# A transformer block on one core: attention starts after 12 projected tiles instead of 16, 22 weight pieces instead of 6 are quantised beside the attention, and the network runs 5 units behind instead of 2

## The chip, the cores and the metric

The kernel runs on one core of one Trainium2 chip. A core has TensorE (PE, the matrix multiplier), VectorE (DVE), ScalarE (ACT), GpSimd (POOL) and SyncE (SP, which here only issues transfers), and each works through its own list of instructions strictly in order; a list stops where an instruction waits for a semaphore. The metric is the device time of one execution in microseconds (us). Three runs of the kernel before took 4254.81, 4255.48 and 4258.41 us; their median, 4255.48 us, is the number that the change is measured against.

## The reference, cut to what matters

For each of 8 sequences of 1024 tokens with 512 features, the layer norm of x feeds two branches whose results are added to x: causal attention with 16 heads of 32 features, and a gated network whose weights and activations are rounded to a 4-bit grid in blocks of 16.

```python
def fp4_linear(x, w):                      # both sides rounded blockwise
    return jnp.einsum('bsk,nk->bsn', fp4_quant_dequant(x), fp4_quant_dequant(w))

def fp4_quant_dequant(x):                  # blocks of 16 along the last dim
    scale = jnp.maximum(jnp.max(jnp.abs(xb), axis=-1, keepdims=True) / 6.0, 1e-12)
    xn = xb / scale
    return grid[searchsorted(mid, abs(xn))] * sign(xn) * scale

xn = layernorm(x)
q, k, v = split(xn @ W_attn + b_attn)      # 512 -> 3 * 512, 16 heads of 32
att = softmax(where(causal, q @ k.T * 32 ** -0.5, -inf))
a = (att @ v) @ W_proj + b_proj
h = silu(fp4_linear(xn, w_gate)) * fp4_linear(xn, w_up)   # 512 -> 1408
out = x + a + fp4_linear(h, w_down)                       # 1408 -> 512
```

## The kernel before

The 8192 tokens are 64 tiles of 128 tokens, 8 to a sequence. The attention of a sequence is 8 units of two heads, so there are also 64 units. Five kinds of work exist, each a generator of small steps:

- `prepare(n)` and `project` (L412 to L532) take a pair of tiles: four transposes each, q and k in four steps (L466) and v in two (L511). q and k are split by DVE into a high and a low part (L491, L492) and stored to memory.
- `maxima(un)` (L557) computes the scores of a unit (PE L597), their row maxima on DVE (L610 for the masked blocks, L622 for the others) and the row sums of the exponentials on ACT (L568). It ends in one small transpose on PE (L655), of which there is exactly one per unit, and in a round trip through memory (L663, L676) that brings the shifts back for `weigh`.
- `weigh(un)` (L682) computes the scores again transposed, takes their exponential on ACT (L735) and multiplies by v (PE L706). While it runs, `maxima` of the next unit runs beside it.
- `network(tiles)` (L785) takes the quantised tile through the gate and up products (L831), SiLU on ACT (L843), the product and the rounding on DVE (L848 and `Quantised`, L267 to L345), transposes (L351) and the down product (L809).
- `finish(tl)` (L914) applies the output projection (L936) to a tile whose whole sequence is through attention, and stores the result.

The network's weights need the same rounding once, before the first tile of the network. They are cut into `PIECES` = 34 pieces of 128 rows by 512 or 384 columns; `weights_quantised` (L357) loads a piece (L367), rounds it on DVE in ten instructions (L335 to L344), turns it on PE (L351) and copies it on ACT (L352).

No engine order is left to a scheduler: `merge` (L1010) takes steps from several `Stream`s in turn and so writes one fixed order for every engine. Each stream has a position that runs with the work done, in units of attention; `merge` picks among the streams that are less than 0.6 units ahead of the last one, with a small model of the engines' costs, to see which could start now. The start is two such merges: the first eight tiles beside weight pieces, then further tiles beside weight pieces and the maxima of unit 0, in the second merge after the loads of units 0 and 1 (`load_half`, 32 transfers at L540, and `load_values`, L552) have been put on SP's list. The third merge holds everything else: unit n at position n, preparations from position 0 on, the network of tile n at position n + `LAG`, `finish` of tile n at n + `LAST` = n + 10. The weight pieces that are left over stand at positions 0 to `LAG` on the network's own stream, ahead of its first tile.

Three constants set the start: `AHEAD` (L76), the number of tiles projected before the third merge; `LAG` (L77); and `EARLY` (L1052), the number of pieces quantised before the third merge. Tiles below `AHEAD` use weights that stay in the chip for that time (L1069 to L1083); later ones fetch them again through a ring of two buffers (`ring_a`, L243).

Of the kernel before, what the change touches and what calls it, by code (L numbers as in the profile page):

```python
# [27 lines left out]
def kernel(  # L28
# [38 lines left out]
    NT = S // P  # L67
# [5 lines left out]
    assert NU == NT  # L73
    QG = 4
    W = QG * P
    AHEAD = 2 * NT  # L76
    LAG = 2  # L77
    LAST = NT + 2
    SOONER = 0.3
    QUEUE = 2.0  # L80
# [76 lines left out]
    def dve(us, after=0.0):  # L157
        return on("dve", us, after)
# [16 lines left out]
    def passed(us):  # L175
        end = clock[0] + us
        while True:
            due = [e for e in waiting_list if e.due <= end]
            if not due:
                break  # L180
            first = min(due, key=lambda e: e.due)
            waiting_list.remove(first)
            clock[0] = max(clock[0], first.due)
            first.now()
        clock[0] = end
# [56 lines left out]

    ring_a = Ring(p2, "wa", wa_in, (B * NT - AHEAD) // QT * 3 * D // (2 * P))  # L243
    ring_p = Ring(p1, "wp", wp_in)
# [112 lines left out]
    def weights_quantised():  # L357
        pieces = []
        for src, dst in ((w_gate, wgT), (w_up, wuT), (w_down, wdT)):
            rows, cols = src.shape  # L360
            for r in range(0, rows, P):
                for c in range(0, cols, CW):
                    pieces.append((src, dst, r, c, min(CW, cols - c)))

        def load(src, dst, r, c, w):
            raw = p3.tile([P, CW], F32, name="hid")[:, :w]
            nc.sync.dma_start(out=raw, in_=src[r : r + P, c : c + w])  # L367
            return raw

        loaded = [load(*piece) for piece in pieces[:3]]  # L370
        done = []
        yield 0.0, clock[0] + 4.0, 0
        for k, piece in enumerate(pieces):
            raw = loaded.pop(0)
            done.append((piece, Quantised(raw, piece[4], raw)))
            while len(done) > (1 if k + 1 < len(pieces) else 0):
                (_, dst, r, c, w), wq = done.pop(0)
                yield from wq.wait()
                transposed(dst[:, c // P : (c + w) // P, r : r + P], wq.done(), w // P)
                if len(pieces) > k + 2:  # L380
                    loaded.append(load(*pieces[k + 2]))
                yield 0.11 * w / P, 0.0, 0, 0.5
# [5 lines left out]
    def load_tokens(tl):  # L388
        tl.xt = p2.tile([P, D], F32, name="xt")
        nc.sync.dma_start(out=tl.xt, in_=x[tl.b, tl.t * P : (tl.t + 1) * P, :])  # L390

    def normed(tl):

        xt = tl.xt
        stats = p4.tile([P, 6], F32, name="stats")
        mv = p4.tile([P, 2], F32, name="mv")
        rstd = p4.tile([P, 1], F32, name="rstd")
        nc.vector.bn_stats(stats, xt)
        nc.vector.bn_aggr(mv, stats)
        nc.vector.tensor_scalar_add(rstd, mv[:, 1:2], EPS)  # L400
        nc.gpsimd.tensor_tensor(rstd, rstd, power, ALU.pow)
        end = pool(0.6, dve(1.1))

        def apply():
            nc.vector.tensor_scalar(xt, xt, mv[:, 0:1], rstd, ALU.subtract, ALU.mult)
            tl.ready = dve(0.57)
            tl.xn = dram.tile([P, D], F32, name="xn_kept", bufs=AHEAD + LAG + 4)
            tl.kept = Later(tl.ready - clock[0] + 0.5, lambda: nc.sync.dma_start(out=tl.xn, in_=xt))

        tl.applied = Later(end - clock[0] + HOP, apply)  # L410

    def prepare(n):  # L412
# [14 lines left out]
        for i, tl in enumerate(tiles[n + QT : n + 2 * QT]):  # L427
            Later(0.5 + i, lambda tl=tl: load_tokens(tl))
            Later(6.0 + 2 * i, lambda tl=tl: normed(tl))
        yield from project(batch, xnT, pair[0].t // QT, end, n < AHEAD)  # L430

    stored = []

    def settle(entries):
        while entries:
            entries.pop(0).now()
# [595 lines left out]
    def up_to(steps, total, over=[0.0]):  # L1032

        total += over[0]
        spent = 0.0
        if steps in said_last:
            yield (0.0,) + said_last[steps]
        while spent < total:
            said = next(steps, None)
            if said is None:  # L1040
                said_last.pop(steps, None)
                return
            said_last[steps] = said[1:3]
            spent += said[-1] if len(said) > 3 else said[0]
            yield said
        over[0] = total - spent
# [2 lines left out]

    N = B * NT  # L1050
    PIECES = sum((w.shape[0] // P) * -(-w.shape[1] // CW) for w in (w_gate, w_up, w_down))
    EARLY = PIECES - 6  # L1052
    tiles = [Tile(n) for n in range(N)]
    units = [Unit(n) for n in range(N)]
    batches = []
# [2 lines left out]
    with tc.manual_schedule(  # L1058
        engines={
            mybir.EngineType.PE,  # L1060
            mybir.EngineType.Activation,
            mybir.EngineType.DVE,
            mybir.EngineType.Pool,
            mybir.EngineType.SP,
        }
    ):
        for tl in tiles[:QT]:
            load_tokens(tl)
        for k in range(2 * NC):  # L1069
            w = p8.tile([P, NC, P], F32, name="pr")  # L1070
            nc.sync.dma_start(out=w, in_=wa_in[:, :, k * P : (k + 1) * P])
            resident_a.append(w)
        nc.sync.dma_start(out=bqk, in_=b_attn[0 : 2 * D].rearrange("(s c p) -> p s c", p=P, c=NC))
        nc.vector.tensor_scalar_mul(bqk[:, 0, :], bqk[:, 0, :], SCALE)
        passed(3.0)
        for tl in tiles[:QT]:
            normed(tl)

        weights_steps = weights_quantised()
        for col in range(2 * D, 3 * D, 2 * P):  # L1080
            w = p2.tile([P, NC, 2 * P], F32, name="wa")
            nc.sync.dma_start(out=w, in_=wa_in[:, :, col : col + 2 * P])
            resident_a.append(w)  # L1083
        part, late = EARLY * 0.25, [0.0]

        def prepared(first, last):
            return itertools.chain(*(prepare(n) for n in range(first, last, QT)))

        merge(
            [  # L1090
                Stream([(prepared(0, NT), 10.8 * NT, 0.0, 1.0)]),
                Stream([(up_to(weights_steps, part, late), part, 0.0, 1.0)]),
            ]
        )
        settle(stored)
        ring_p.load()
        for n, h in ((0, 0), (0, 1), (1, 0), (1, 1)):
            load_half(units[n], h)
        load_values(units[0])
        net = network(tiles)  # L1100
        TILE = sum(4 * 1.72 * w / CW + w / P * 0.97 for _, w in chunks)

        def first_maxima():
            yield 0.0, clock[0] + 6.0, 1
            yield from maxima(units[0])

        merge(
            [
                Stream([(prepared(NT, AHEAD), 10.8 * NT, 0.0, 1.0)]),
                Stream([(up_to(weights_steps, part, late), part, 0.0, 1.0)]),  # L1110
                Stream([(first_maxima(), 6.0, 0.3, 0.7)]),
            ]
        )
        ring_a.load()
        ring_a.load()
        load_biases()

        def last_weights():
            for half in range(2):
                wp = p2.tile([P, NC, 2 * P], F32, name="wa")  # L1120
                nc.sync.dma_start(out=wp, in_=wp_in[:, :, half * 2 * P : (half + 1) * 2 * P])
                resident.append(wp)
            yield 0.0, 0.0, 0

        def networks():
            yield weights_steps, (PIECES - EARLY) * 0.5, 0.0, LAG
            for n in range(N):
                yield up_to(net, TILE), TILE, n + LAG, 1.0

        def preparations():  # L1130
            for n in range(AHEAD, N, QT):
                yield prepared(n, n + QT), 10.8 * QT, n - AHEAD, QT
            yield last_weights(), 1.0, N - AHEAD + 1, 0.0

        merge(
            [
                Stream((weigh(un), 17.5, un.n, 1.0) for un in units),
                Stream((maxima(un), 6.0, un.n - 1 - SOONER, 1.0) for un in units[1:]),
                Stream(networks()),
                Stream((quantised(tl), 0.45, tl.n + LAG - 1, 0.5) for tl in tiles),  # L1140
                Stream(preparations()),
                Stream((finish(tl), 4.5, tl.n + LAST, 1.0) for tl in tiles),
            ]
        )
        passed(100.0)
# [37 lines left out]
```

## Time and profile before

One execution was taken by the profiler. It is not one of the three timed runs.

| what | value |
|---|---|
| median of 3 runs | 4255.48 us |
| the profiled execution, its own time | 4251.42 us |
| its span, first to last instruction | 4249.7 us |
| PE busy | 4131.2 us, 97% |
| DVE busy | 2763.2 us, 65% |
| ACT busy | 2321.8 us, 55% |
| mean granted TensorE clock | 0.991 |
| first statistics transpose (L655) starts | 272.7 us |
| first `weigh` of unit 0 (L724) starts | 290.8 us |
| last weighted product (L706) ends | 4127.2 us |

How to read it: the busy time of an engine is the time in which it has an instruction under way; ends of matmuls are modelled, so a busy PE is not PE at its best rate. The 40 slices of the page are 106 us each. The windows view gives, for a stretch of time, the busy time of each engine with the number of its instructions, the granted TensorE clock and the share of the transfer engines' time. The timeline merges equal instructions that follow each other; a bracket holds the engine's idle time before them and what ended it. The 64 statistics transposes (L655) cut the span into 65 stages, numbered 0 to 64 below: stage 0 is everything up to the first one, stage 64 everything after the last.

### The profile page before, as it was taken

To read this page: it belongs to the slowest core of one execution; us is meant where nothing else is said; L and a number is where in the kernel's file an instruction comes from. 1 tells how busy PE (TensorE), PEld (TensorE's weight loads), DVE (VectorE), ACT (ScalarE), POOL (GpSimd) and SP (SyncE) were. 2 spreads that over 40 slices of the span, in tenths; PEclk is the share of its full clock that TensorE was granted. 3 is DMA by queue.
4 is the path that set the end of the run, shared out by engine and by line. 5 is a ranking of instruction groups with operands and counts; after the bars stand their busy time and mean duration, and the time that the engine had idled before them with its cause. 6 is when DMAs were issued, how large, how long until landed. Compare 5 with 4: busy or idle time off the path is not lost.

```text
span 4249.7 us, 58555 instructions
## 1 busy us (share of the span) xinstructions
PE 4131.2 (97%) x17684; PEld 2619.1 (62%) x17684; DVE 2763.2 (65%) x7323; ACT 2321.8 (55%) x5918; POOL 546.5 (13%) x1296
## 2 busy tenths in 40 slices
PE   7789999999999999999999999999999999999998
PEld 6666666666666666666666666666666555555555
DVE  6786765666575666575666575666565666667755
ACT  2246556565555565555565555565555666666640
POOL 0001111111111111111111111111111111111110
PEclk9889999999999999999999999999999999999999
DMA  5654434455455455455455455455454433333314
GB/s 183 177 173 129 124 103 120 118 157 157 132 155 150 140 164 153 132 156 151 140 160 155 134 154 149 141 162 153 138 149 131 117 92 94 95 92 93 93 56 126
DMA packets 564187, 573.84 MB, mean 135 GB/s; under 512 B 114976, under 2 KB 420128, under 8 KB 563872
## 3 DMA queue, kind: packets, MB, share of 16 engines
q1 hardware_dynamic: 563872, 570.10, 48.3%
q8 instruction: 142, 2.33, 0.2%
q14 instruction: 173, 1.42, 0.1%
HBM read 400.56 MB, written 169.35 MB: 134 GB/s over the span
## 4 chain that ended last, share of the span: by engine, by line
PE 82%; ACT 7%; DVE 4%; DMA 1%; issue 1%; SPq 0%; ACTq 0%; POOL 0%; DVEq 0%
PE bank L831 26%; PE acc L809 12%; PE bank L466 8%; PE y L706 7%; PE bank L724 6%; PE bank L727 6%; PE bank L597 5%; PE bank L936 5%; PE bank L511 4%; ACT bank L568 3%; PE bank L351 2%; ACT L568 1%; ACT L843 1%; ACT pr L735 1%; DMA ks<-y_kept 1%
## 5 line engine op out<-in xcount | busy, mean ns | idle before, releaser
L568 ACT ACTIVATE bank<-bank,neg 128x512 f32<-128x512 f32 (+3 forms) x1536 | 856.7, 559 | 163.7 <-DVE neg L610 119.8
L735 ACT ACTIVATE pr<-bank 128x512 f32<-128x512 f32 (+3 forms) x1536 | 662.7, 494 | 482.6 <-PE bank L727 478.2
L741 POOL TENSOR_SCALAR_AFFINE_SELECT pr<-pr 128x128 f32<-128x128 f32 x1024 | 393.2, 397 | 3238.3 <-ACT pr L735 3228.9
L610 DVE CUSTOM_DVE_ANT_0 bank<-bank,mask 128x128 f32<-128x128 f32 (+3 forms) x1024 | 501.2, 500 | 469.5 <-PE bank L597 455.7
L724 PE MATMUL bank<-shT,pick 128*128 128x512 f32 (+3 forms) x1536 | 683.8, 453 | 2.7 <-DVE hid L848 1.5
L831 PE MATMUL bank<-wuT,xqT 128*128 128x512 f32 (+1 forms) x1536 | 676.1, 565 | 3.9 <-ACT bank L568 1.0
L809 PE MATMUL acc<-wdT,hqT 128*128 128x512 f32 x1408 | 665.4, 596 | 1.3 <-ACT hqT L352 1.3
L831 PE MATMUL bank<-wgT,xqT 128*128 128x512 f32 (+1 forms) x1536 | 662.9, 561 | 0.0
L597 PE MATMUL bank<-ks,qs 128*128 128x512 f32 (+3 forms) x1536 | 636.2, 475 | 24.7 <-ACT bank L568 21.7
L727 PE MATMUL bank<-qs,ks 128*128 128x512 f32 (+3 forms) x1536 | 516.9, 346 | 0.0
L622 DVE TENSOR_REDUCE neg<-bank 128x1 f32<-128x512 f32 x512 | 345.7, 685 | 186.8 <-PE bank L597 185.6
L597 PEld LDWEIGHTS bank<-ks,qs 128*128 128x128 f32 x1536 | 277.5, 191 | 234.1 <-issue 111.3
L831 PEld LDWEIGHTS bank<-wuT,xqT 128*128 128x128 f32 x1536 | 277.0, 190 | 228.8 <-issue 158.9
L831 PEld LDWEIGHTS bank<-wgT,xqT 128*128 128x128 f32 x1536 | 280.0, 190 | 219.3 <-issue 151.9
L724 PEld LDWEIGHTS bank<-shT,pick 128*128 128x128 f32 x1536 | 290.4, 189 | 155.7 <-issue 78.9
L809 PEld LDWEIGHTS acc<-wdT,hqT 128*128 128x128 f32 x1408 | 255.3, 190 | 197.0 <-issue 183.6
L478 ACT ACTIVATE full<-bank,bqk 128x256 f32<-128x256 f32 x256 | 107.4, 470 | 491.1 <-PE bank L466 409.3
L727 PEld LDWEIGHTS bank<-qs,ks 128*128 128x128 f32 x1536 | 290.6, 189 | 110.6 <-issue 77.1
L466 PE MATMUL bank<-xnT,wa 128*128 128x256 f32 x1536 | 349.8, 381 | 0.9 <-ACT xnT L352 0.6
L466 PEld LDWEIGHTS bank<-xnT,wa 128*128 128x128 f32 x1536 | 288.4, 190 | 55.6 <-issue 18.9
L706 PE MATMUL y<-pr,vs 128*32 128x512 f32 (+3 forms) x3072 | 316.5, 501 | 0.8 <-POOL pr L741 0.8
L568 ACT ACTIVATION_READ_ACCUMULATOR bank<-bank,neg 128x1 f32 x1536 | 315.4, 205 | 0.0
(99 smaller groups left out, 4674.7 us busy)
## 6 DMA issues: line engine op xcount, KB each, us to landing
wa<-in_L_attn_W_attn_dram SPq DMA_DIRECT2D x146, 512.0 KB
qs<-qk_kept SPq DMA_DIRECT2D x512, 128.0 KB
ks<-qk_kept SPq DMA_DIRECT2D x512, 128.0 KB
wp<-in_L_attn_W_proj_dram SPq DMA_DIRECT2D x81, 512.0 KB
qk_kept<-high SPq DMA_DIRECT2D x128, 256.0 KB
qk_kept<-full SPq DMA_DIRECT2D x128, 256.0 KB
y_kept<-yu SPq DMA_DIRECT2D x256, 128.0 KB
yT<-y_kept SPq DMA_DIRECT2D x112, 256.0 KB
```

Of the source, the lines that this page charges most:

```text
L466: nc.tensor.matmul(pq[:, j, :], lhsT=halves[j][:, c, :], rhs=xnT[:, c, :], start=(c == 0), stop=(c == NC - 1),)
L568: nc.scalar.activation(part, part, AF.Exp, bias=neg[:, kind, k + j : k + j + 1], scale=1.0 if kind == 1 else -1.0, accum_out=sums[:, kind, ...
L597: nc.tensor.matmul(sc[:, j * n : (j + 1) * n], lhsT=un.qs[Q][:, r, i * P : (i + 1) * P], rhs=un.ks[h][:, r, :n], start=True, stop=True,)
L610: nc.vector.tensor_tensor_reduce(part, part, mask[:, W - n :], scale=-1.0, scalar=3e38, op0=ALU.add, op1=ALU.min, accum_out=neg[:, kind, k ...
L622: nc.vector.tensor_reduce(neg[:, kind, k : k + 1], sc[:, :n], AX.X, ALU.max, negate=True)
L706: nc.tensor.matmul(y[row : row + HD, q0:], lhsT=un.vs[h][:, jj, r * HD : (r + 1) * HD], rhs=pr[:, q0:], start=(j < 2), stop=(j >= last - 1 ...
L724: nc.tensor.matmul(w[:, q0:], lhsT=pick[:, Q * HU + r, :], rhs=un.shT[:, q0:], start=True, stop=False)
L727: nc.tensor.matmul(w[:, q0:], lhsT=un.ks[h][:, r, jj * P : (jj + 1) * P], rhs=un.qs[Q][:, r, q0:], start=False, stop=True,)
L735: nc.scalar.activation(pr[:, q0:], w[:, q0:], AF.Exp)
L741: nc.gpsimd.affine_select(out=pr[:, q0 : q0 + P], in_=pr[:, q0 : q0 + P], compare_op=ALU.is_ge, fill=0.0, base=0, pattern=[[1, P]], channe ...
L809: nc.tensor.matmul(tl.acc, lhsT=job.hqT[:, j, :], rhs=wdT[:, i, :], start=(i == 0), stop=(i == NI - 1))
L831: nc.tensor.matmul(job.g, lhsT=job.tl.xqT[:, c, :], rhs=wT[:, c, job.i0 : job.i0 + job.w], start=(c == 0), stop=(c == NC - 1),)
```

## The change

`AHEAD` goes from 16 to 12, `LAG` from 2 to 5 and `EARLY` from 28 to 12. The two merges of the start take their share of the early pieces by tiles instead of half each, so 8 of the 12 pieces stand beside the first eight tiles and 4 beside the next four. The ring of projection weights, whose count depends on `AHEAD`, then serves two more pairs of tiles, and the memory buffers of normalised tiles (`AHEAD + LAG + 4`) go from 22 to 21. Nothing else is changed.

```diff
-    AHEAD = 2 * NT
-    LAG = 2
+    AHEAD = 12
+    LAG = 5
...
-    EARLY = PIECES - 6
+    EARLY = PIECES - 22
...
-        part, late = EARLY * 0.25, [0.0]
+        part, late = EARLY * 0.5 / AHEAD, [0.0]
...
                 Stream([(prepared(0, NT), 10.8 * NT, 0.0, 1.0)]),
-                Stream([(up_to(weights_steps, part, late), part, 0.0, 1.0)]),
+                Stream([(up_to(weights_steps, part * NT, late), part * NT, 0.0, 1.0)]),
...
-                Stream([(prepared(NT, AHEAD), 10.8 * NT, 0.0, 1.0)]),
-                Stream([(up_to(weights_steps, part, late), part, 0.0, 1.0)]),
+                Stream([(prepared(NT, AHEAD), 10.8 * (AHEAD - NT), 0.0, 1.0)]),
+                Stream([(up_to(weights_steps, part * (AHEAD - NT), late), part * (AHEAD - NT), 0.0, 1.0)]),
                 Stream([(first_maxima(), 6.0, 0.3, 0.7)]),
```

## The prediction

> **What bounds the kernel now.** I read the page first, then the busy time by stages, then the timelines of the engines at the two ends of the span. The page:
>
> ```profile
> PE 4131.2 (97%) x17684; PEld 2619.1 (62%) x17684; DVE 2763.2 (65%) x7323; ACT 2321.8 (55%) x5918; POOL 546.5 (13%) x1296
> ...
> PE   7789999999999999999999999999999999999998
> ...
> DVE  6786765666575666575666575666565666667755
> ...
> PEclk9889999999999999999999999999999999999999
> ```
>
> PE is the bound over the whole, but not in the first three slices, where it is busy for seven or eight tenths and its clock is below full. Only those slices, and the last, leave something to win. The stages, cut where the statistics transposes (L655) start:
>
> ```profile
> core 0: us, PE busy (x) PEld busy (x) DVE busy (x) ACT busy (x) POOL busy (x), PEclk, DMA share, GB/s
> 0.00:272.70 272.70, 205.65 (x967) 177.31 (x967) 206.58 (x484) 73.76 (x174) 14.72 (x34) 0.91 0.58 176
> 272.70:322.60 49.90, 44.20 (x193) 30.43 (x193) 37.83 (x110) 29.13 (x85) 5.50 (x16) 0.88 0.62 179
> 322.60:358.80 36.20, 33.15 (x150) 22.54 (x150) 24.68 (x76) 25.08 (x78) 4.13 (x15) 0.91 0.53 140
> 358.80:419.80 61.00, 59.41 (x272) 36.87 (x270) 35.05 (x97) 40.15 (x103) 10.70 (x29) 0.97 0.41 117
> 921.60:1049.40 127.80, 127.31 (x550) 80.73 (x549) 81.14 (x219) 72.07 (x184) 17.11 (x40) 1.00 0.54 149
> 4127.20:4208.60 81.40, 74.57 (x219) 38.35 (x220) 43.95 (x91) 9.99 (x17) 2.53 (x2) 1.00 0.26 79
> 4208.60:4249.70 41.10, 31.11 (x129) 24.85 (x127) 16.17 (x31) 0.00 (x0) 0.00 (x0) 0.96 0.76 215
> 290.80:332.70 41.90, 40.06 (x200) 27.05 (x199) 40.32 (x110) 28.86 (x84) 7.04 (x20) 1.00 0.70 201
> ```
>
> Stage 0 (first row) is DVE's: 206.6 us busy against some 189 us of matmuls, if these are counted at the spacing of their starts at full clock (a 128x512 one 0.43 us, a 128x256 one 0.215 us, as in the timeline). Stages 1 and 2, attention without the network, fill no engine on PE's side. Two units with everything in them take 127.8 us (fifth row), of which PE is busy 127.3. From stage 3 on each us of PE work is a us of time. The last row of the fence is the stretch in which DVE is densest, 40.3 of 41.9 us.
>
> One stall in stage 0 decides what follows. VectorE's and SyncE's timelines:
>
> ```profile
> 162.21 0.69 DVE L398 BATCH_NORM_STATS2 stats<-xt 128x6 f32<-128x512 f32 x1 [14.06 <-DMA xt<-in_L_attn_x_dram]
> ```
>
> ```profile
> 138.21 1.90 SPq L540 DMA_DIRECT2D qs<-qk_kept  x4
> ...
> 156.36 0.93 SPq L552 DMA_DIRECT2D vs<-v_kept  x2
> 157.54 0.95 SPq L390 DMA_DIRECT2D xt<-in_L_attn_x_dram  x2
> ```
>
> Between the two merges SP issues 32 loads of units 0 and 1 one after the other (18.2 us), and the next tiles' x queues behind them; DVE, in order, waits 14 us for it. From the first L540 to the arrival it is 24.0 us.
>
> **The change, part by part.** The changed program has the same matmuls and DVE instructions in another order; 20 more loads of 512 KB (12 for the four tiles now projected through the ring, 8 of the output weights), and eight loads fewer of activation tables. I count its instructions by stage and price DVE's at their mean by form: a 512-wide piece is ten instructions, 0.679 + 0.178 + 0.353 + 0.181 + 0.683 + 0.430 + 0.432 + 0.687 + 0.701 + 0.686 = 5.0 us; the maxima of a unit 4 x (0.297 + 0.433 + 0.570 + 0.701) + 16 x 0.141 + 8 x 0.685 = 15.7; its statistics 2.2; a split of q or k 1.13; the norm of a tile 1.56. Neighbours overlap a little: stage 1 sums to 44.3 and was busy 37.8, stage 2 to 29.1 and 24.7, so true need is 0.85 of these sums.
>
> *Stage 0.* Before: 29 pieces, 18 norms, 32 splits, one unit's maxima: 227.8 by means, 272.7 us long. After: 13 pieces (65), 14 norms (22), 24 splits (27), maxima and the rest (20): 134; PE's work falls from 189 to 139, so the two are level. Eight tiles were through PE at 120.4 before; with about five transposed pieces fewer (0.44 us each) I take 118. SP's list no longer has two piece loads waiting for DVE there (before, L540 began 14.7 us after the last store of v), so the 32 loads start at 119.8, and x lands 24.0 us later, at 143.8. Behind that point DVE has 42 us left by means, and before, 111 us by means behind the same point took 110: 186. Bounds: 180 (DVE at its 0.85) and 200 (PE late by the 11.7 us it lost at this place before). **186, a gain of 87.**
>
> *Stages 1 to 6*, in place of 321.5 us, are the units without network. After, DVE has 50.8, 39.2, 48.8, 39.7, 41.7 and 33.4 by means (5, 4, 5, 4, 3 pieces in the first five), PE only 33, 29, 30, 29, 30 and 40 of work, ACT 37 to 39 by means, of which 0.78 was busy in stages 1 and 2. So DVE leads, and pieces that stood beside projections now stand beside maxima. Stage 1: 50.8 x 0.85 = 43.4, and the 12.1 us that DVE was idle in this stage before (10.8 of it for the bias product, L257, which keeps its place): 55.5. Stages 2 to 5: 169.4 x 0.85 = 144.8 busy. Bounds: 0.96 dense, as in the last row of the fence, 150.8; or 11.5 us idle in each, as in stage 2 before (36.2 - 24.7), 190.9. The dense row is the nearest, as it holds four pieces in one unit; but in two of the four stages the list has nothing between L637 and L641, where DVE waited 6.0 us for ACT in stage 2. 150.8 + 12 and a little: 165. Stage 6 is PE's, 39.6 of work and 4 over it: 43.5. **Together 264, 57 less than before, with 84 us less of PE work done.**
>
> *Stages 7 to 63* are bound by PE. They gain two pairs of projections (41.3 us and their transposes) and lose 7.3 of network: 34.1 of work. The pattern by which units alternate changes, 58.2 and 63.5 us of PE work per stage instead of 66.8 and 55.0; the sum of a pair is the same, and the excess of time over work (3.0 per stage) came with blocks of score products, of which there are as many. Bounds +-8 us. **3485.5 + 34.1 = 3519.6.** The added loads lie under PE, where the transfer engines were half busy (0.54); POOL, which masks and adds the bias, was busy 17 of 127.8 us and follows its units.
>
> *Stage 64*, after the last statistics, takes over 99.8 us of PE work, 93 of it network: three more tiles have no attention beside them. In 4127.2 to 4208.6 the network alone lost 8 us of 81 (6.8 of it idle), waiting for rounded activations:
>
> ```profile
> 4175.39 0.55 PE L351 MATMUL bank<-ident,hid 128*128 128x128 f32 x3 [0.93 <-DVE hid L344]
> ...
> 4199.92 0.66 PE L351 MATMUL bank<-ident,hid 128*128 128x128 f32 x4 [2.06 <-DVE hid L344]
> ```
>
> 3.4 us of that are the drain at the end, once in either case; 4.8 on 70 makes 7 us for the 100 added. Against it, eight `finish` at the end, 4.8 us apart for 3.45 of PE work, become four and a half: 4 us back. **170.0 + 99.8 + 3 = 273** (bounds 266 and 285).
>
> **Sum.** 186 + 264 + 3520 + 273 = 4243 for the span, 6.5 under 4249.7. The profiled execution's own time is 1.7 over its span and 4.1 under the median; the same shift gives 4249 us, 0.15% less than 4255.48. About 0.2%, 8.5 us, is what a measurement of this kernel can tell from no change, so this is a forecast of no difference: 87 and 57 won, 34 and 103 given back.
>
> *A rule against the change.* In 336 to 350 us the clock was 0.76 of full, though PE's longest listed wait there was 0.3 us; units without network run at 0.90. The Trainium skill ("TensorE: Matmul & The Clock Gate", Part 1) has the clock halved after an idle window of about 3.4 us. By the rule alone the five units, whose PE waits are short, would keep the full clock; by the row their 30 us of PE work become 33. Both stay under DVE's need, so the sum is the same by either.
>
> **The rivals.**
>
> *Slower: DVE idles in the units without network as it did in stage 2.* For it: maxima pass PE, DVE and ACT in turn, DVE is in order, and ACT has two rows of exponentials to do. Against it: the dense row, and a list in which pieces stand between the maxima. Four stages at 48 instead of 41 are +26: span 4269, time 4275. It turns slower than measurable once DVE idles more than 8.8 us per unit ((165 + 15 - 144.8) / 4).
>
> *Faster: these units run dense to the end.* Stages 2 to 5 at 150.8 and stage 1 with 2 less, stage 0 at DVE's lower bound: -22, time 4227. For it, 40.3 busy of 41.9; against it, the 6.0 us wait at L641 and every stage with a different mix.
>
> *The start shortens less.* The 32 loads keep their place between the merges and the lists now put the first score products among the projections of tiles 8 and 9; PE too, in order, could stop there. 200 for stage 0: time 4263, 0.2% slower.
>
> *The tail is worse than before's.* If each of the eight chunk pairs without attention waits 3 us more, as the worst one did (2.06): +20, time 4269.
>
> **How the numbers follow.** No measurable change 0.33, the dense case 0.35 (with all between), DVE idling 0.20, the start 0.06, the tail 0.06. The last three are the slower side, 0.32. The range goes from just under the dense case, 4224, to past the slower ones, 4284; the likeliest case's own is 4247 to 4264.
>
> **What would show it.** The first L655 near 186 us and x of tile 10 arriving near 144, with a DVE wait of some 15 us before it; six stages of about 55, 38, 46, 39, 41 and 44, DVE over nine tenths busy in 2 to 5; pairs of stages of 127.8 us later on; the last statistics near 3970, 273 from the end, with under 5 `finish` after the last down product. The forecast is wrong if DVE in stages 2 to 5 shows idle times over 9 us each (slower) or under 2 (faster), or if the later pairs differ from 127.8 by more than 0.3 us.

## The result and the profile after

The changed kernel takes 4295.92 us (median; 4292.55 to 4299.85) against 4255.45 us of the kernel before, a ratio of 1.0094 with a 95% interval of 1.0077 to 1.0112. It is 0.94% slower; the forecast was 4249 us, no measurable difference, and its range ended at 4284. The profiled execution has a span of 4296.8 us, 47.1 more than the one of before; by the medians the change costs 40.5, because before's profiled execution was 4.1 us under its median and the one of after (4298.54 us) 2.6 over its own. The accounts by stages below go by the spans.

The page of the kernel after, the same lines as were shown of before:

```profile
PE 4185.4 (97%) x17684; PEld 2626.3 (61%) x17684; DVE 2793.2 (65%) x7323; ACT 2312.0 (54%) x5910; POOL 538.9 (13%) x1296
...
PE   8789999999999999999999999999999999999999
...
DVE  6588666566666575666575666675666576666565
...
PEclk9899999999999999999999999999999999999999
```

On this page nothing looks wrong: the first slice is fuller than before, the last one too, and PE is busy 97% as before. PE is busy 54 us longer for the same 17684 matmuls, and that is the only sign. The view by stages says where. It is the windows view of the kernel after, cut at the starts of the statistics transposes (columns: stretch, length, busy time of PE, of weight loads, DVE, ACT and POOL with the number of instructions, granted clock, transfer share, GB/s):

```profile
0.00:188.20 188.20, 148.58 (x697) 127.17 (x697) 119.44 (x291) 54.33 (x134) 13.38 (x30) 0.95 0.64 193
188.20:246.40 58.20, 47.89 (x214) 32.14 (x214) 44.04 (x120) 31.43 (x89) 7.75 (x20) 0.88 0.59 164
246.40:289.20 42.80, 39.60 (x189) 26.09 (x189) 33.94 (x95) 29.13 (x85) 6.43 (x18) 0.96 0.58 155
289.20:334.20 45.00, 41.18 (x192) 26.51 (x192) 42.17 (x117) 30.68 (x89) 8.23 (x20) 0.96 0.68 185
...
374.10:416.90 42.80, 38.20 (x176) 26.15 (x176) 35.84 (x103) 28.50 (x84) 4.80 (x14) 0.92 0.66 178
416.90:467.90 51.00, 48.50 (x195) 27.94 (x193) 31.61 (x86) 31.23 (x85) 7.13 (x19) 0.90 0.37 94
1120.50:1249.60 129.10, 128.16 (x549) 80.71 (x548) 82.87 (x218) 72.13 (x184) 16.76 (x40) 1.00 0.53 148
1249.60:1380.50 130.90, 129.96 (x550) 81.94 (x550) 82.87 (x219) 72.13 (x184) 16.76 (x40) 0.99 0.54 146
4027.90:4296.80 268.90, 255.53 (x849) 140.72 (x847) 147.79 (x314) 44.87 (x84) 17.49 (x33) 0.98 0.26 77
```

Against the prediction's four stretches:

| stretch | before, us | predicted | after | missed by |
|---|---|---|---|---|
| stage 0 | 272.7 | 186 | 188.2 | +2.2 |
| stages 1 to 6 | 321.5 | 264 | 279.8 | +15.8 |
| stages 7 to 63 | 3485.5 | 3519.6 | 3559.9 | +40.3 |
| stage 64 | 170.0 | 273 | 268.9 | -4.1 |

The two ends came as forecast. Three quarters of the miss lies in the long middle, for which the prediction named no rival. Two full units take 129.1 us there (the row from 1120.50), and every third pair 130.8 (the row from 1249.60, to the nearest tenth), where before had 127.8 each time. PE is busy 128.16 of 129.10 us in them: the loss shows as busy time, not as idle time.

PE's matmuls are the same before and after, so the time can be split into PE's work and the rest. Work counts each matmul at the spacing of starts at full clock, as in the prediction (a pair of score products of 512 columns 0.23 us each). The rest, called loss below, is idle time, half clock and waits that show as busy (the trace can list a matmul as under way while it waits):

| loss, us | before | after | change |
|---|---|---|---|
| stage 0 | 84.1 | 49.4 | -34.7 |
| stages 1 to 6 | 46.8 | 89.2 | +42.4 |
| stages 7 to 63 | 179.7 | 220.0 | +40.3 |
| stage 64 | 24.4 | 23.5 | -0.9 |
| all | 335.0 | 382.1 | +47.1 |

The 34.7 us saved in the start are lost again, and more, in the units without network; the middle loses another 40.3 for a reason of its own.

### The profile page after: what moved, and what is told of

Same layout as the page of the kernel before. It is cut to its first block, busy times and chain, and to the rows that moved or that the text cites. A ratio compares the mean times of both kernels' runs of the same rounds, so it can differ in the third digit from the quotient of the medians.

```text
span 4296.8 us, 58607 instructions
## 1 busy us (share of the span) xinstructions
PE 4185.4 (97%) x17684; PEld 2626.3 (61%) x17684; DVE 2793.2 (65%) x7323; ACT 2312.0 (54%) x5910; POOL 538.9 (13%) x1296
## 5 line engine op out<-in xcount | busy, mean ns | idle before, releaser
L568 ACT ACTIVATE bank<-bank,neg 128x512 f32<-128x512 f32 (+3 forms) x1536 | 859.9, 562 | 149.8 <-DVE neg L610 125.8
L610 DVE CUSTOM_DVE_ANT_0 bank<-bank,mask 128x128 f32<-128x128 f32 (+3 forms) x1024 | 502.4, 499 | 535.7 <-PE bank L597 315.2
L741 POOL TENSOR_SCALAR_AFFINE_SELECT pr<-pr 128x128 f32<-128x128 f32 x1024 | 381.7, 387 | 3203.8 <-ACT pr L735 3194.4
L724 PE MATMUL bank<-shT,pick 128*128 128x512 f32 (+3 forms) x1536 | 655.0, 435 | 3.1 <-ACT bank L568 1.8
L831 PE MATMUL bank<-wgT,xqT 128*128 128x512 f32 (+1 forms) x1536 | 653.3, 560 | 2.9 <-DVE res L941 0.2
L622 DVE TENSOR_REDUCE neg<-bank 128x1 f32<-128x512 f32 x512 | 345.7, 685 | 191.6 <-PE bank L597 190.9
L466 PE MATMUL bank<-xnT,wa 128*128 128x256 f32 x1664 | 389.7, 388 | 3.5 <-ACT bank L568 1.4
L466 PEld LDWEIGHTS bank<-xnT,wa 128*128 128x128 f32 x1664 | 318.6, 194 | 70.2 <-ACT bank L568 15.9
L568 ACT ACTIVATION_READ_ACCUMULATOR bank<-bank,neg 128x1 f32 x1536 | 318.7, 208 | 0.0
## 6 DMA issues: line engine op xcount, KB each, us to landing
qs<-qk_kept SPq DMA_DIRECT2D x512, 128.0 KB
ks<-qk_kept SPq DMA_DIRECT2D x512, 128.0 KB
y_kept<-yu SPq DMA_DIRECT2D x256, 128.0 KB
```

Source lines behind the costliest of these rows:

```text
L466: nc.tensor.matmul(pq[:, j, :], lhsT=halves[j][:, c, :], rhs=xnT[:, c, :], start=(c == 0), stop=(c == NC - 1),)
L568: nc.scalar.activation(part, part, AF.Exp, bias=neg[:, kind, k + j : k + j + 1], scale=1.0 if kind == 1 else -1.0, accum_out=sums[:, kind, ...
L610: nc.vector.tensor_tensor_reduce(part, part, mask[:, W - n :], scale=-1.0, scalar=3e38, op0=ALU.add, op1=ALU.min, accum_out=neg[:, kind, k ...
L622: nc.vector.tensor_reduce(neg[:, kind, k : k + 1], sc[:, :n], AX.X, ALU.max, negate=True)
L724: nc.tensor.matmul(w[:, q0:], lhsT=pick[:, Q * HU + r, :], rhs=un.shT[:, q0:], start=True, stop=False)
L741: nc.gpsimd.affine_select(out=pr[:, q0 : q0 + P], in_=pr[:, q0 : q0 + P], compare_op=ALU.is_ge, fill=0.0, base=0, pattern=[[1, P]], channe ...
```

## The experiments

**First theory: the middle depends on whether `LAG` is even.** Preparations come in pairs of tiles and so repeat every two units. The network of tile n stands at n + `LAG`; with an odd `LAG` the even tile's network meets the other half of a preparation. The rival was that fewer tiles ahead (another phase of the projections and their loads) made the pairs longer.

*lag4*: the kernel after with

```diff
-    LAG = 5
+    LAG = 4
```

> The changed kernel with the network four units behind instead of five; 12 tiles and 22 pieces stay. Theory (the parity of the lag sets the order of the full units: with an even lag a pair of units is written in the same order as before the change): two full units take 127.8 us again instead of 129.1 to 130.9, the clock has no half-rate window in them, and the time is 4250 to 4265 us. Rival (the shorter lead of 12 tiles makes the full units slower, whatever the lag): 129 to 131 us for two units, time 4285 to 4300.

Measured: 4262.9 us, ratio to before 1.0020 (1.0010 to 1.0029), as the theory had it. The pairs take 127.8 us, loss in stages 7 to 63 is 178.8.

*prep_shift*: the kernel after, `LAG` 5, with the preparations one unit later

```diff
-                yield prepared(n, n + QT), 10.8 * QT, n - AHEAD, QT
+                yield prepared(n, n + QT), 10.8 * QT, n - AHEAD + 1, QT
```

> The changed kernel with lag 5, but each pair of tiles from the 13th on prepared one unit later. Theory (what counts is the place of the network relative to the preparation, two units being one period of both): the order of the full units is that of before, 127.8 us for two, time 4250 to 4265. Rival (the odd lag is bad against the units themselves, or the 12 tiles are): 129 to 131 us, time 4285 to 4300.

Measured: 4265.5 us, 1.0024 (1.0014 to 1.0034), half a us over the theory's range and far from the rival's. Pairs of 127.8 (two of 128.0 and 128.1), loss in stages 7 to 63 182.5. So it isn't the number 5, nor the distance of the network: it is how network and preparations stand to each other.

*lag3_only*: the kernel before with

```diff
-    LAG = 2
+    LAG = 3
```

> The kernel before with the network three units behind instead of two and nothing else: 16 tiles ahead, 6 pieces beside the attention. Theory (parity): two full units take 129.1 to 130.9 us, some 18 pairs at 2 us more, so time 4285 to 4300, slower by 0.7 to 1%. Rival (the 12 tiles or the late pieces make the full units slower): 127.8 us for two, time 4250 to 4265.

Measured: 4290.9 us, 1.0087 (1.0072 to 1.0102). Pairs of 129.1 (one of 130.8), loss in stages 7 to 63 212.5, with the 16 tiles and 28 pieces of before in the start. So the smaller number of tiles ahead isn't needed for it. By these three it is shown that parity is worth 33 to 41 us in the middle: 220.0 against 178.8 and 182.5 with the start of after, 212.5 against 179.7 with that of before. The miss there was 40.3.

**Second question: what does PE wait for in the odd order?** The timeline of PE in the kernel after, in the pair at 1120 (first line) and in the next, one of those of 130.8 us:

```profile
1148.00 3.72 PE L466 MATMUL bank<-xnT,wa 128*128 128x256 f32 x16
...
1272.68 1.02 PE L809 MATMUL acc<-wdT,hqT 128*128 128x512 f32 x2
1273.54 0.60 PE L351 MATMUL bank<-ident,xs 128*128 128x128 f32 x4
1274.43 1.95 PE L597 MATMUL bank<-ks,qs 128*128 128x384 f32 x4 [0.29 <-ACT bank L568]
1276.56 0.49 PE L597 MATMUL bank<-ks,qs 128*128 128x512 f32 x1 [0.17 <-DMA xn_kept<-xt]
1277.12 5.41 PE L466 MATMUL bank<-xnT,wa 128*128 128x256 f32 x16
```

Five score products in a row; from the transposes at 1273.54 to the projection at 1277.12 there are 3.58 us, where the matmuls need some 1.5. The listed idle times are 0.29 and 0.17 us only. A bank is one of the buffers into which PE writes its results; in this kernel a matmul takes it again only when the engine that reads it is through. ScalarE's timeline of the same place has the reason for the wait for L568:

```profile
1271.70 0.59 ACT L769 COPY yu<-y 128x512 f32<-128x512 f32 x1 [2.99 <-PE y L706]
1272.31 1.28 ACT L568 ACT_TABLE_LOAD   x1
1273.60 0.66 ACT L568 ACTIVATE bank<-bank,neg 128x512 f32<-128x512 f32 x1
```

ACT stands 2.99 us idle at L769, a copy of the weighted sums that PE has yet to finish; behind it, in order, come a table load and then the exponentials that set score banks free. Summed over every run of score products in stages 18 to 29 (excess over their work, per pair), this one run loses 2.04 us after; the costliest of before (four products, behind two table loads and two SiLU) 1.05, and no other run more than 0.4 in either.

*no_table* and *no_table_before*: is it the table load? Both leave SiLU out.

```diff
-            nc.scalar.activation(job.hid, job.g, AF.Silu)
+            nc.scalar.activation(job.hid, job.g, AF.Identity)
```

> The kernel after, same order, with the identity in place of SiLU at L843, so that ScalarE need not load another table between the network and the exponentials; this leaves out SiLU. Theory that the 1.28 us table load makes the bunched score products of the odd order wait: pairs of two full units fall from 129.1 (130.8 every third) to within 0.5 us of what no_table_before shows. Rival, that the order of PE's work itself costs it (bunched products waiting for VectorE and ScalarE and the clock): the pairs stay 1 us or more above those of no_table_before.

> The kernel before with the identity in place of SiLU at L843, as the counterpart of no_table; this leaves out SiLU. If the table loads cost anything in the even order, its pairs fall under 127.8 us; by both theories they fall by under 0.5, since PE is busy 127.3 of 127.8 there.

Measured, one execution each: 4249.16 us and 4218.09. Pairs 128.1 in the odd order, 126.6 in the even one: a gap of 1.5, so the rival's side by the number. The load is worth the same in both, 1.0 us of a pair of 129.1 and 1.2 of one of 127.8, and both theories missed the second: they had it under 0.5, since PE is busy 127.3 of 127.8 us there. What went altogether in the odd order is the pair of 130.8: no half-rate stretch is left in stages 7 to 63.

*yu_dve* and *yu_dve_before*: take L769 off ScalarE, in the odd order and in the even one.

```diff
-            nc.scalar.copy(yu, y)
+            nc.vector.tensor_copy(yu, y)
```

> The kernel after, same order, with the copy of the weighted sums (L769) on VectorE instead of ScalarE. In its later pairs one run of five score products (L597, behind the transposes of xs) costs 2.0 us more than its matmuls: it waits for banks from L568, and ScalarE stands there in order at L769, idle for 2.99 us, with the table load of L568 behind it. Theory (this wait is what the odd order loses): ScalarE loads the table in that idle time, the pairs fall from 129.1 and 130.8 to 127.9 to 128.3, the half-rate windows go, stages 13 to 48 take 2296 to 2310 us instead of 2332.9, and the time is 4258 to 4275. Rival (another wait comes last there, VectorE's or PE's own): the pairs stay over 128.8 and the time at 4288 or more.

> The same edit in the kernel before. Its costly run of score products (1.05 us a pair) waits behind two table loads and two SiLU, with no L769 among them. Theory: pairs stay at 127.8 within 0.2 and the time at 4245 to 4260. Rival, that L769 on ScalarE costs PE time anywhere: pairs fall by about 1 here too and the time is under 4235.

Measured: yu_dve 4265.8 us, 1.0026 (1.0017 to 1.0035) of before, 30 us under the kernel after. Every pair takes 128.1, stages 13 to 48 take 2305.0 us, no half-rate stretch between 447 and 3662 us. yu_dve_before 4257.0, 1.0003 (0.9993 to 1.0012), pairs of 127.7 and 127.8. All as the theory had it. PE's timeline of yu_dve at the same place:

```profile
1271.82 0.60 PE L351 MATMUL bank<-ident,xs 128*128 128x128 f32 x4
1272.18 1.42 PE L597 MATMUL bank<-ks,qs 128*128 128x384 f32 x4
1273.78 0.50 PE L597 MATMUL bank<-ks,qs 128*128 128x512 f32 x1 [0.18 <-ACT bank L568]
1274.34 1.99 PE L466 MATMUL bank<-xnT,wa 128*128 128x256 f32 x8
```

and ScalarE's:

```profile
1267.01 1.28 ACT L568 ACT_TABLE_LOAD   x1
1268.30 0.66 ACT L568 ACTIVATE bank<-bank,neg 128x512 f32<-128x512 f32 x1
```

The table load now falls into the time in which ScalarE was idle. The first exponential after it begins 3.5 us before the transposes (1268.30 and 1271.82), not 0.06 after them (1273.60 and 1273.54), and from the transposes to the projection it is 2.52 us instead of 3.58: 1.06 less a pair, and with it the half clock is gone. The run now loses 0.98 beyond its work, as much as the costliest run of before. Loss in stages 7 to 63 is 185.7 instead of 220.0.

no_table says what part the load has in it. There ScalarE stands at L769 as long as in the kernel after, but no load follows; its line, and PE's two:

```profile
1261.10 0.59 ACT L769 COPY yu<-y 128x512 f32<-128x512 f32 x1 [2.99 <-PE y L706]
```

```profile
1262.95 0.60 PE L351 MATMUL bank<-ident,xs 128*128 128x128 f32 x4
...
1265.46 0.70 PE L466 MATMUL bank<-xnT,wa 128*128 128x256 f32 x2
```

From the transposes to the projection it is 2.51 us here, and the pairs take 128.1 as in yu_dve. So what delays the run is the wait and the load behind it together; either can be taken away. The gap to no_table_before stays because the costliest run of before stands behind table loads too and goes with them: no run there loses more than 0.4. In all, 34 of the 40.3 us went with L769's move off ScalarE, some 8.5 of them as half clock (five pairs that were 1.7 longer). The 0.3 us by which a pair is still longer than in the even order were not taken apart.

**Third question: why do stages 1 to 6 lose 42 us, and what is a move of pieces or tiles worth alone?**

*ahead12_only*: the kernel after with `LAG` and `EARLY` of before, so that only the four tiles move, and with them the shares of the pieces: some 19 of the 28 stand beside the first eight tiles, 14 before.

```diff
-    LAG = 5
+    LAG = 2
...
-    EARLY = PIECES - 22
+    EARLY = PIECES - 6
```

> Attention begins after 12 tiles; the lag of 2 and the 6 late pieces are those of before. Theory (parity): full units at 127.8 us for two; the start is bound by VectorE with 28 pieces beside 12 tiles and gains little, time 4245 to 4265. Rival (the shorter lead costs in the full units): 129 us or more, time 4280 to 4300.

Measured: 4284.4 us, 1.0070 (1.0055 to 1.0085); pairs 127.8, as the theory had it, but the time is 19 us over its range. It lies in the rival's range, whose reason the pairs rule out. The windows view of its start:

```profile
0.00:265.80 265.80, 170.31 (x763) 144.06 (x763) 194.39 (x462) 64.00 (x151) 12.68 (x30) 0.82 0.51 154
```

42.6 us of PE work less, and the start is only 6.9 us shorter (272.7 before): DVE has its 28 pieces all the same, and the clock falls to 0.82. DVE isn't busy throughout either (194.39 us): it waits 25.8 us for pieces to be loaded, 14.5 in the start of before.

*early22_only*: the kernel before with the pieces alone moved, into two units as `LAG` stays 2.

```diff
-    EARLY = PIECES - 6
+    EARLY = PIECES - 22
```

> The kernel before with one part of the change alone: 12 early pieces instead of 28, so that 22 stand in stages 1 and 2 (VectorE 82.0 and 76.3 us by means there); 16 tiles ahead, LAG 2. Start: PE's 178 us and some 50 over it, 230 instead of 272.7. If the two units are bound by VectorE's work they take about 82 and 70, and stages 0 to 4 together 489 instead of 472: time 4268 to 4278 us. If a piece costs as little here as in the start: 4258 or less. If the chain through ScalarE adds 10 us or more per unit: 4288 or more.

Measured: 4297.2 us, 1.0095 (1.0080 to 1.0110). The start is 49.4 us shorter (223.3), stages 1 and 2 are 91.7 longer (96.3 and 81.5 instead of 49.9 and 36.2). The first of them:

```profile
223.30:319.50 96.20, 58.09 (x258) 40.49 (x256) 70.64 (x181) 35.96 (x97) 9.82 (x20) 0.78 0.47 134
```

DVE is busy 70.64 of 96.2, and the 0.85 of its means, on which both the prediction and the expectation rested (82.0 x 0.85 = 69.7), is right as busy time. But 25 us of the stage are none of it. The third branch of the expectation holds by its time and not by its reason: none of DVE's listed waits in this stage is for ScalarE. They are 10.3 us for the bias product (10.8 in the same stage of before), 4.1 for pieces to be loaded, and one that the stage of before doesn't have, for the load of the bias:

```profile
DVE inv_y L251 <- DMA bv<-in_L_attn_b_attn_dram: 9.9, 1, 9.9
```

In stage 2 DVE is busy 65.35 of 81.5 us and waits 7.4 for score products and 4.8 for pieces.

*light_pieces*: the kernel after, same order, without four of the ten DVE instructions of a piece (L325, L328, L342, L343), those that round the weights.

```diff
-            return [
+            return self.kept([
...
+        def kept(self, steps):
+            n = len(steps) if not self.light else 3
+            return steps[:n] + [(*each[:3], lambda: None) for each in steps[n:6]] + steps[max(n, 6):]
...
-            done.append((piece, Quantised(raw, piece[4], raw)))
+            done.append((piece, Quantised(raw, piece[4], raw, light=True)))
```

> The kernel after, in the same order of instructions on every engine, with the four instructions of each weight piece that form the step of the grid and round to it taken away from VectorE (six of ten are left); this leaves out the rounding of the network's weights. By means VectorE has 39.5, 30.1, 37.9, 31.5 and 35.3 us in stages 1 to 5 in place of 50.8, 39.2, 48.8, 39.7 and 41.7. Theory that VectorE's work sets these stages: stages 2 to 5 (170.6 us in the kernel after) fall by 25 to 30, to 141 to 146, and stage 0 falls too. Rival, that the chain from PE through VectorE and ScalarE and back sets them, with the clock: they fall by under 10 us, to 161 or more.

Measured, one execution: 4281.5 us, 14 under the kernel after. Stages 2 to 5 take 158.2 instead of 170.5, 12.3 less; neither branch, but nearer the rival's 161 than the 146 of the theory. Two of the four rows:

```profile
284.60:324.50 39.90, 37.07 (x192) 25.70 (x192) 32.80 (x97) 30.75 (x89) 6.67 (x20) 1.00 0.77 209
324.50:363.80 39.30, 36.61 (x189) 24.53 (x189) 26.93 (x85) 29.00 (x85) 4.63 (x18) 1.00 0.66 174
```

Of 30.9 us less of DVE busy time (146.4 to 115.6) four tenths came back. All four units now take 38.8 to 40.2 us, however much of that DVE is busy (26 to 33), so it isn't DVE's work that sets them any more. DVE's listed waits in them are 23.0 us for PE's score products (L610, L622) and 13.1 for ACT at L641; in the kernel after they are 9.9 and 7.8. What sets the units, presumably the way of a unit's scores through PE, DVE and ACT and back, was not found out. Some of the 12.3 can be the clock: it is 1.00 in all four stages here, and 0.96, 0.96, 1.00 and 0.92 after, which is at most 6.9 us (0.04 x 42.8 + 0.04 x 45.0 + 0.08 x 42.8, if PE was on the path all that time).

**Last: the change turned round.** If tiles beside DVE's pieces are cheap, more of them belong in the start, with `LAG` even.

*ahead20*: `AHEAD` 20, the rest as before (its fractions of pieces taken by tiles as after).

```diff
-    AHEAD = 12
-    LAG = 5
+    AHEAD = 20
+    LAG = 2
...
-    EARLY = PIECES - 22
+    EARLY = PIECES - 6
```

> The kernel after with LAG 2, 28 early pieces and 20 tiles projected ahead: against the kernel before, only AHEAD goes up by four where the change took it down by four. ahead12_only moved 42.6 us of PE work out of the start and shortened it by only 7 us, because VectorE kept its pieces. Theory (the start is VectorE's, and each tile projected beside it brings some 10.8 us of PE work for little of VectorE's): the start has 231 us of PE work and 243 us of VectorE work by means, so it grows from 272.7 to about 282, and 43 us leave the later stages: 4222 to 4230 us, pairs of later stages at 127.8 as LAG is even. Rival (the start is bound by the chain from loads through PE to VectorE and back, each tile costs its PE time): the start grows by 35 to 43 us, to 310 or so, and the time stays at 4250 to 4260.

Measured: 4231.9 us, 0.9949 (0.9932 to 0.9966) of before, 2 us over the expected range. Its start:

```profile
0.00:285.80 285.80, 242.85 (x1175) 211.69 (x1175) 224.65 (x515) 84.27 (x198) 17.98 (x38) 0.96 0.63 192
```

13.1 us longer than before's for 43 us more of PE work, with the clock at 0.96 instead of 0.91; the loss in stage 0 falls from 84.1 to 54.2. The shares of the pieces moved too (some 11 beside the first eight tiles instead of 14), and DVE's 14.5 us of waiting for pieces to be loaded are gone; what each of these is worth was not taken apart.

*ahead24* (`AHEAD` 24, otherwise as ahead20):

> As ahead20, with 24 tiles projected ahead. VectorE's work in the start stays (241 us by means), PE's grows from 231.6 to 253.7, and stage 1 takes 21 us more of PE work and 17 more of VectorE's; 43 us leave the later stages. If PE's work beside VectorE's goes on being nearly free (ahead20: 43 us of it lengthened the start by 13), the start stays under 295 and the time is 4210 to 4220. If the start has become PE's by now, it grows by 22, stage 1 by 21, and the time stays at 4228 to 4236.

Measured: 4231.9 us, 0.9938 (0.9922 to 0.9955). The start is 12.1 longer again, but stage 1 takes 79.2 instead of 52.1: the branch without further gain holds, though it is stage 1 and not the start that gives back the most.

*ahead20_e3* (ahead20 with `EARLY = PIECES - 3`):

> As ahead20, with 31 pieces in the start instead of 28: three pieces, 14 us of VectorE by means, go from stages 1 and 2 to the start. If a piece costs more beside attention without network than beside projections, as the kernel after suggests, stages 1 and 2 lose more than the start takes: 4222 to 4229 us. If it costs its VectorE time in either place: 4230 to 4236.

Measured: 4235.7 us, 0.9955 (0.9940 to 0.9970). Start +9.5, stages 1 to 6 -3.7: three pieces cost no more beside attention than in a start that is full. By the times the two can't be told apart.

*ahead20_yu* (ahead20 with L769 on VectorE):

> ahead20 with L769 on VectorE, as a version that may beat both kernels: its order is the even one, so by the theory it gains little, 4222 to 4236 us; by the rival that L769 costs anywhere, 4195 to 4210.

Measured: 4231.2 us, 0.9942 (0.9927 to 0.9957), as the theory had it: in the even order the copy costs nothing. ahead20, ahead24 and ahead20_yu are 0.5 to 0.6% faster than before and 1.5% faster than after, and can't be told apart.

The losses of the runs side by side, in us (their sums differ by what the spans differ by, within 0.2):

| kernel | stage 0 | 1 to 6 | 7 to 63 | 64 | all |
|---|---|---|---|---|---|
| before | 84.1 | 46.8 | 179.7 | 24.4 | 335.0 |
| after | 49.4 | 89.2 | 220.0 | 23.5 | 382.1 |
| yu_dve | 49.6 | 92.0 | 185.7 | 23.4 | 350.7 |
| lag4 | 49.8 | 97.8 | 178.8 | 22.0 | 348.4 |
| prep_shift | 48.4 | 94.6 | 182.5 | 23.5 | 349.0 |
| lag3_only | 85.1 | 57.4 | 212.5 | 21.2 | 376.2 |
| ahead12_only | 119.8 | 41.9 | 181.8 | 25.5 | 369.0 |
| early22_only | 44.9 | 125.8 | 185.4 | 24.6 | 380.7 |
| ahead20 | 54.2 | 48.9 | 182.9 | 25.2 | 311.2 |

## Why the prediction was wrong

**The step that failed** is "the excess of time over work (3.0 per stage) came with blocks of score products, of which there are as many", with its "bounds +-8 us". The number of blocks is nearly the same, but what a block loses depends on what ScalarE has in its list at that moment. The new order puts a run of five behind L769 and the table load that follows it, and there PE waits: 2.04 us a pair over its work, where no run of before loses more than 1.05. yu_dve takes that one wait away and lands at 3525.6 us in stages 7 to 63, 6.0 over the predicted 3519.6 and inside its bounds. The prediction saw the new pattern of alternation (63.5 and 58.2 of work per stage), and even named the pair of 127.8 as a thing to watch and 0.3 us as the point at which it falls; what it didn't do was to write out ScalarE's and PE's new order of one pair and ask which bank wait comes last in it. The order was known before the run.

**Stage 0** was right as a whole, 188.2 for 186, in part by luck, as two errors cancel. The 32 loads began at 113.48 and not at 119.8, and the tiles' x came at 138.97 after a wait of 17.9 us, forecast 143.8 and some 15. SyncE's and VectorE's timelines of the kernel after:

```profile
113.48 1.97 SPq L540 DMA_DIRECT2D qs<-qk_kept  x4
```

```profile
138.97 0.69 DVE L398 BATCH_NORM_STATS2 stats<-xt 128x6 f32<-128x512 f32 x1 [17.90 <-DMA xt<-in_L_attn_x_dram]
```

From there to the first statistics transpose it took 49.2 us, not the 42 that DVE had left by means. So x came 4.8 us too early and the rest took 7.0 too long; why, was not taken apart.

**Stages 1 to 6** were 15.8 us too short. Stage 1 took 58.2 for 55.5. Stages 2 to 5 took 170.5 for 165: DVE's busy time was right (146.4 for 144.8), its idle time was 24.1, 2.8 to 8.9 a unit. The dense row from which the lower bound came (40.3 of 41.9) was approached in one unit of four (stage 3, 42.17 of 45.00); "DVE over nine tenths busy in 2 to 5" held for stage 3 alone. light_pieces gave back only 0.4 us for each us of DVE's work that it leaves out, some of that perhaps by the clock, so DVE's work was not by itself what set these units, which is how the prediction summed them. Stage 6 missed most, 51.0 for 43.5, and has no pieces at all: it was taken for PE's, but the first tile of the network starts there into an empty chain. In the waits of that stage:

```profile
DVE hid L848 <- PE bank L831: 12.7, 2, 7.5
```

DVE waits twice for the first gate and up products, and the clock is 0.90. light_pieces, with 50.9 in this stage, shows that pieces have no part in it. How the 7.5 us divide was not taken apart: the clock is worth at most 5.1 (0.10 x 51.0), and without SiLU's table loads (no_table) the stage takes 48.6.

**Stage 64** took 268.9 for 273, within its bounds.

Some products in the working are off, without bearing on the result: 50.8 x 0.85 is 43.2 and 169.4 x 0.85 is 144.0, four stages at 48 instead of 41.25 are +27, and eight waits of 3 us are +24, with 2.06 as the worst one shown.

**The rivals.** None of the four is what happened, and none concerned stages 7 to 63, where most of the miss lies. DVE's idling, the nearest by time (4275), stayed under the 8.8 us per unit from which it was to decide, with 6.0; the start and the tail did as forecast; and the dense case didn't come. Had the order been even, the rest of the misses would have made 4263 to 4266 us (lag4, prep_shift), measurably slower by little: within the forecast's range and around the upper end of its likeliest case.

**Where the gain of the start went** is answered by early22_only, ahead12_only and lag4 together. Either part of the start's change alone costs 29 (tiles) or 41 us (pieces). Together, over four units, they cost 7.5 by the medians and 13.6 by the spans: the start loses 34 us less, stages 1 to 6 lose 51 more (97.8 for 46.8). A piece that stands beside attention lengthens a unit that PE can't fill; in before's start the same pieces stood beside projections, and ahead20 shows projections to be nearly free there (13.1 us for 43). The last few pieces are an exception, by ahead20_e3.

The prediction's last term, 6 us from the span to the median, came out at -0.9 for the kernel after (4295.92 against 4296.8), so by spans the forecast was 54 short and by times 47. The two profiled executions lie on different sides of their medians, and no row tells that beforehand.

## What to carry to other kernels

When a change shifts two periodic streams against each other, write out one period of the new order on every engine before calling the steady state unchanged: look for a run of matmuls whose banks are freed by an engine that stands, in order, at a wait for something else. Work that fills one engine should be placed beside work that fills another: here moving projections into the start, where VectorE leads, gained 0.5%, and moving VectorE's pieces out to units that PE can't fill lost what the shorter start had won. And a PE that is busy 99.3% of a pair (128.16 of 129.10) can still take 1% longer for the same work; the time per period tells, not the busy share.

## What the runs showed of the hardware

The clock fell to half in places where PE was hardly idle. In the kernel after this happened at 888, 1277, 1666, 2055 and 2444 us, each time for 3.4 us, at the same place of every third pair: behind the run of score products with listed waits of 0.29 and 0.17 us, the 16 projections of L466 took 5.41 us instead of 3.72. With the waits shortened (yu_dve, no_table) it was gone.

The same run is there in every pair, and only every third was hit, at intervals of 389.1 us. The clock records of this trace have a grid: the half-clock stretches begin whole multiples of 3.413 us from one another (137.20, 188.40, 888.13 and 1277.26 us are 15.0, 205.0 and 114.0 of them apart), and those of the other runs do too. Two pairs of 129.1 us and one of 130.8 are also 389.0, so a pair that was hit brings the run back to nearly the same place on the grid three pairs later. light_pieces, with the same order, has the same interval (1003.20 and 1392.32); lag3_only, with pairs of 129.1, was hit once, at 2804.86. This fits a hit that goes by where the run lies on the grid; how much waiting within one stretch brings it about, no run here settles.

The Trainium skill ("TensorE: Matmul & The Clock Gate", Part 1, "A second HAM failure mode: psum-queue depth-cycling") describes such a case, a PE that is idle for very short times between groups as it goes through its banks and whose clock then swings; the rows agree with that passage, and not with the rule of an idle window of about 3.4 us that the prediction weighed, as the listed idle times before the hit at 1277.26 are 0.46 us together. The same Part has the window run freely with a length of 3.413 us; the grid in the clock records agrees.

A change of activation tables took ScalarE 1.28 us and nothing more: L769 ended at 1272.29, the load ran from 1272.31, the exponential began at 1273.60. The Trainium skill ("ScalarE: Activation LUTs", "What ACT_TABLE_LOAD costs") has 1.283 us for the load, which agrees, and another 1.38 us of draining for each change, which this trace doesn't show.

That the table loads were worth 1.2 us of a pair in the even order, with PE busy 99.6% of it, was not expected either: a score product that waits for its bank can count as busy. In the costliest run of before 1.05 us go beyond the work, and 0.17 us are listed as idle.
